# A recurrent layer and an expert attention on one core: maxima halved over partitions, fewer turns, and a first pass beside the projection

## The chip, the core and the metric

The kernel runs on one core of one Trainium2 chip. The metric is the time of one execution on the device, in microseconds; three executions were taken. One further execution was recorded by the hardware profiler. The engines are PE (matrix multiply, with PEld for its weight loads), DVE (vector), ACT (scalar, activations), POOL (GpSimd) and SP (issues transfers). PE writes to PSUM only, which has eight banks; the other data lies in SBUF. Everything is in float32.

## The reference

Two layers, each on normalised input and added to its input. x has the shape 2 x 2048 x 256 (B, T, D).

```python
# layer 1: a plain recurrent layer, h starts at zero
xi = jnp.einsum('btd,hd->bth', x, Wi) + bi
def step(h, xt):
    h_new = jnp.tanh(xt + h @ Wh.T + bh)
    return (h_new, h_new)
...
# layer 2: attention with experts, H = 8 heads of DH = 64, E = 5 experts, 2 chosen
q = (x @ Wq).reshape(b, t, h, dh).transpose(0, 2, 1, 3)
k = (x @ Wk).reshape(b, t, h, dh).transpose(0, 2, 1, 3)
wv = _topk_mask(gl_v, SEL) * jax.nn.sigmoid(gl_v)
xv = jnp.einsum('btd,edk->btek', x, Wv)
v = jnp.einsum('bthe,btek->bhtk', wv, xv)
scores = jnp.einsum('bhid,bhjd->bhij', q * scale, k)
probs = jax.nn.softmax(scores, axis=-1)
attn = jnp.einsum('bhij,bhjd->bihd', probs, v)
out = jnp.einsum('bthe,bthk,ekd->btd', mask_o, attn, Wo)
...
x = x + _L0_attn_ref(_layernorm(x, axis=-1), ...)
x = x + _L0_ffn_ref(_layernorm(x, axis=-1), ...)
```

## The kernel before

**The recurrent layer.** The 2048 steps of a sequence are cut into 128 segments (NS) of 16 steps (S), which run side by side: chunk c holds step c of every segment, for both sequences (B = 2). `measure` takes the norms (DVE), `turn_in` normalises a chunk (POOL) and turns it on PE, `project_in` multiplies it by Wi on PE and writes it with the biases to `xi` (ACT); the input dimension has two halves (KC = 2), so a chunk has two tiles `px`. The loop at L322 puts these in an order written out by hand. Then come two runs over the steps. Run "a" starts every segment from zero at step 3 (SKIP) and keeps only the end states, `ends`; step 3 itself has no matrix product. Run "b" starts every segment from the end state of the one before it, keeps all states in `hs`, and has the residual, the norms and the turning back of the layer beside it (`beside`). In both, `step` (L355) treats the two sequences apart: four products of 128 columns each in two halves, an add of `xi` on DVE, a tanh on ACT. `compare` checks that run b's end states agree with run a's to four units in the last place; if not, a flag makes the kernel run a slow pass over everything.

**The attention.** A unit is one head with 512 queries (QB): 64 units, each in U_T = 4 turns of the loop over T at L1154, each turn with two tiles t of 256 keys (HC = 8 tiles per unit). `scores` writes a tile's scores, 128 x 2 x 512, to two PSUM banks (ps_s, two buffers); `stage` copies them to SBUF (ACT); `largest` takes the running maximum over the tiles (DVE) into `m`. At a unit's seventh tile (c = HC - 2) it folds the two halves of the 256 keys together: `half` in PSUM, then `mm`, 128 x 512 (L663 to L666). What is left is a maximum over 128 partitions: `turn_max` turns `mm` on PE in four pieces, `reduce_max` reduces each (DVE, L684), `spread_max` turns the result back to all partitions on PE (`pt`, L693), and ACT copies it to SBUF (`top`, L699). `subtract` takes it off the staged scores, on DVE from PSUM for a unit's first two tiles, on POOL from SBUF for the other six; `exponential` is ACT; `products` multiplies with the values into the bank `o`; `fold` adds two tiles by a transfer from POOL's queue; `sums` takes the sum over the keys into bank `d`. The subtraction lags the scores by LAG - 1 = 5 turns, the products by 6.

In a turn the engines' order is the order of the calls: exponential of an old tile, scores of two new ones, stage and maximum of each, the subtractions (`fresh` marks the turn with a unit's first two, `sub`), then what the table `before` holds for this turn, the products, the sums, an exponential, and the tables `first_behind` and `behind`; the table `between` is called between the stages and the maxima. `take` brings a finished unit's products to SBUF (ACT copy, DVE add): it is called at the start of the turn after the unit's last products. `close`, `gather` and others finish the unit; `keys` and `queries` of the next head come in `before`, in every unit's third turn.

The values are mixed from five experts per token: `first_experts` projects them for sequence 0 (PE, ACT copy out of a bank: `misc`, which has two buffers, and the bank "d" in turn), `mix` weighs them with the gates and `mix_sum` adds them up (DVE); `experts` projects them for sequence 1 during an earlier head.

Of the kernel before, what the change touches and what calls it, by code (L numbers as in the profile page):

```python
# [14 lines left out]
P = 128  # L15
# [5 lines left out]
def pass_over(  # L21
# [237 lines left out]

    S = NCH  # L260
    NS = P
    NEWTON = 3


# [8 lines left out]

    with tile_pool(name="prep", bufs=3) as pp, tile_pool(
        name="lna", bufs=3
    ) as lnp, tile_pool(name="ps_xi", bufs=3, space=PSUM) as ps_xi, tile_pool(
        name="ps_t", bufs=3, space=PSUM
    ) as ps_t, tc.manual_schedule():
        norm_of, turned = {}, {}

        def measure(c0, n):
            mv = pp.tile([P, n * B, 2], F32, tag=f"mv{n}", name=f"mva{c0}")
            for c in range(c0, c0 + n):
                for b in range(B):
                    stats(lnp, mv[:, (c - c0) * B + b, :], xt[c][:, b, :], f"a{c}_{b}")
            neg, y = scales(lnp, mv, n * B, f"a{c0}")
            for c in range(c0, c0 + n):
                norm_of[c] = neg, y, (c - c0) * B

        def turn_in(c):  # L290
            neg, y, k = norm_of.pop(c)
            xn = pp.tile([P, B, D], F32, tag="xn", bufs=2, name=f"xn{c}")
            tp = ps_t.tile([P, KC, B, P], F32, tag="tp", name=f"tpa{c}")
            for b in range(B):
                normalize(xn[:, b, :], xt[c][:, b, :], neg, y, k + b)
                for kc in range(KC):
                    nc.tensor.transpose(tp[:, kc, b, :], xn[:, b, kc * P : (kc + 1) * P], ident)
            turned[c] = pp.tile([P, KC, B, P], F32, tag="xnT", bufs=2, name=f"xnT{c}")
            nc.scalar.copy(turned[c], tp)

        def project_in(c):
            xnT = turned.pop(c)
            for mc in range(KC):
                px = ps_xi.tile([P, B, P], F32, tag="px", name=f"px{c}_{mc}")
                for kc in range(KC):
                    nc.tensor.matmul(  # L306
                        px.rearrange("p b n -> p (b n)"),
                        lhsT=wi[:, kc, mc * P : (mc + 1) * P],
                        rhs=xnT[:, kc].rearrange("p b n -> p (b n)"),
                        start=kc == 0,  # L310
                        stop=kc == KC - 1,
                    )
                nc.scalar.activation(xi[:, mc, c], px, AF.Identity, bias=bsum[:, mc : mc + 1])

        groups, c0 = [], 0
# [26 lines left out]

    TOL = 4 * 2.0**-23
    GC = NCH // 2
    SKIP = 3
# [6 lines left out]

    def step(nm, s, prev, h, ps_h):  # L355
        for b in range(B):
            if prev is None:
                for mc in range(KC):
                    nc.scalar.activation(h[:, mc, b, :], xi[:, mc, s, b, :], AF.Tanh)
                continue  # L360
            pre = sp.tile([P, KC, NS], F32, tag=f"pre{b}", name=f"pre{nm}_{s}_{b}")
            for mc in range(KC):
                ph = ps_h.tile([P, NS], F32, tag=f"ph{b}_{mc}", name=f"ph{nm}_{s}_{b}_{mc}")
                for kc in range(KC):
                    nc.tensor.matmul(  # L365
                        ph,
                        lhsT=wh[:, kc, mc * P : (mc + 1) * P],
                        rhs=prev(kc, b),
                        start=kc == 0,
                        stop=kc == KC - 1,  # L370
                    )
                nc.vector.tensor_tensor(pre[:, mc, :], ph, xi[:, mc, s, b, :], ALU.add)
                nc.scalar.activation(h[:, mc, b, :], pre[:, mc, :], AF.Tanh)  # L373

    def run(nm, from_zero, keep_states, ps_h, beside=None):
        prev = None if from_zero else (lambda kc, b: ends[:, kc, b, 0:NS])
        for s in range(SKIP if from_zero else 0, S):
            if keep_states:
                h = hs[:, :, s]
            elif s == S - 1:  # L380
                h = ends[:, :, :, 1:]
            else:
                h = sp.tile([P, KC, B, NS], F32, tag="h", name=f"h{nm}_{s}")
# [132 lines left out]
    with tile_pool(name="ps_h", bufs=1, space=PSUM) as ps_h:  # L516
        if slow:
            nc.gpsimd.memset(hs[:, :, S - 1], 0.0)
            with tc.For_i(0, NS, 1):
                nc.vector.tensor_copy(ends[:, :, :, 1:], hs[:, :, S - 1])  # L520
                run("c", False, True, ps_h)
            for c in range(S):
                turn_back(c, "c")
                add_back(c, nc.gpsimd)
# [69 lines left out]
    def first_experts(c):  # L594
# [9 lines left out]
        nc.scalar.copy(xq[:, c % 4], pv.rearrange("p e k -> p k e"))  # L604
        if c % 4 == 3:
# [47 lines left out]
    def largest(t, ss):  # L653
# [8 lines left out]
        half = misc([P, QB], f"mh{u}")  # L662
        nc.vector.tensor_tensor(half, ss[:, 0, :], m[:, 0, :], ALU.max)  # L663
        nc.vector.tensor_tensor(m[:, 1, :], ss[:, 1, :], m[:, 1, :], ALU.max)
        mm_of[u] = ap.tile([P, QB], F32, tag="mm", bufs=1, name=f"mm{u}")
        nc.vector.tensor_tensor(mm_of[u], half, m[:, 1, :], ALU.max)  # L666
        m_of.pop(u)


# [3 lines left out]
        return spare["pool"].tile([P, QB], F32, tag="z", name=nm)  # L673

    def turn_max(u):
        pm = misc([P, QS, P], f"pm{u}")
        mm = mm_of.pop(u)
        for s in range(QS):
            nc.tensor.transpose(pm[:, s, :], mm[:, s * P : (s + 1) * P], ident)
        mx_of[u] = (pm, ap.tile([P, QS], F32, tag="mq", name=f"mq{u}"))  # L680

    def reduce_max(u):
        pm, mq = mx_of[u]
        nc.vector.tensor_reduce(mq, pm, AX.X, ALU.max)  # L684

    def spread_max(u):
        _, mq = mx_of[u]
# [282 lines left out]

    before, between, first_behind, behind = {}, {}, {}, {}

    def at(table, T, f, *a):
        table.setdefault(T, []).append(lambda: f(*a))

# [8 lines left out]
    for i, (b, h) in enumerate(heads):  # L984
# [10 lines left out]
        at(before, T0 + 2, queries, i, 1)  # L995
        for part in range(4):
            if i == 0:
                at(behind, (3, 5, 6, 7)[part], mix, i, part)
                at(behind, (3, 5, 6, 7)[part], mix_sum, i, part)
            else:  # L1000
                T = T0 + U_T * (part - 2) + 2
                at(behind, T - 2, fetch, i, part)
# [1 line left out]
                at(before, T + 1, mix_sum, i, part)  # L1004
        if h == H - 3 and b + 1 < B:
            for c in range(NCH):
                T = T0 + c // 2 * U_T + 1
                at(before if c % 2 else behind, T + c % 2, experts, b + 1, c)
    for b in range(1, B):

# [9 lines left out]
        for c in range(NCH):  # L1020
            T = T0 + c // 2 * U_T + c % 2
            at(behind, T - 2, load_late, b, c)
            at(behind, T, normalize_late, b, c)
            at(behind, T + 2, turn_late, b, c)
            at(behind if c % 2 else before, T + 3, logits_late, b, c)
        T0 += 2 * NCH + U_T
        for part in range(2):
# [15 lines left out]
    for u, (i, n) in enumerate(units):  # L1043
# [10 lines left out]
        if h == H - 1 and (n < NQ - 3 or b < B - 1):  # L1054
            T = T1 + LAG + 4
            for tab, t, f, o, *more in PLACES:
                if T + t < NT:
                    at(tab, T + t, f, b, n * QS + o, *more)

    def drain():  # L1060

# [91 lines left out]
    with tc.manual_schedule():  # L1153
        for T in range(NT):  # L1154
            new = (2 * T, 2 * T + 1)
            sub = [t for t in (2 * (T - LAG + 1), 2 * (T - LAG + 1) + 1) if 0 <= t < 2 * NT]
            old = [t for t in (2 * (T - LAG), 2 * (T - LAG) + 1) if 0 <= t < 2 * NT]
            u_old = (T - LAG) // U_T - 1
            done = (T - LAG) % U_T == 0 and 0 <= u_old < len(units)
            fresh = sub and sub[0] % HC == 0  # L1160
            if done:
                take(u_old)
            if old:
                exponential(old[1])

# [10 lines left out]
            else:  # L1176
# [92 lines left out]
```

## Time and profile before

| | us |
|---|---|
| Three executions | 1551.83, 1552.19, 1552.85 |
| Their median | 1552.19 |
| The profiled execution, its own time | 1552.41 |
| Its span, first to last instruction | 1550.6 |

The mean granted clock of PE was 0.999 of full speed. The page of the profile gives, of the span, how long each engine was busy; a busy PE isn't PE at its peak. These groups of the page belong to the change (line, engine, operation, tiles and shapes, count; busy time and mean ns of one; idle time of the engine just before them and what ended most of it):

```profile
L706 POOL TENSOR_TENSOR p<-p,top 128x1024 f32<-128x1024 f32 x378 | 1009.6, 2780 | 26.2 <-ACT top L699 25.9
L660 DVE TENSOR_TENSOR m<-s,m 128x1024 f32<-128x1024 f32 x320 | 390.9, 1222 | 83.4 <-PE s L638 73.9
L706 DVE TENSOR_TENSOR p<-p,pt 128x1024 f32<-128x1024 f32 x126 | 152.5, 1210 | 0.0
```

By stage, from the time line: the projection runs from 9 to 52 us, run a from 53 to 75, run b to 111, and the first scores come at 121.5. The first unit's maxima are turned at 157.8 and the last one's at 1499.3, which is 21.3 per unit on the mean; the rest is the last units' finish.

### The profile page before, as it was taken

What the parts mean: (1) busy time and instruction counts of PE and PEld (TensorE: products, weight loads), DVE (VectorE), ACT (ScalarE), POOL (GpSimd) and SP (SyncE); (2) the same over time, 40 slices, a digit from 0 to 9 for tenths busy, and PEclk for the clock granted to TensorE, in tenths of its full rate; (3) what the DMA queues carried; (4) which work ended last, traced back from release to release, by engine and by line L of the source; (5) the groups of instructions that cost most, each with busy time, mean ns of one, the idle gap of its engine ahead of it and who ended that gap; (6) DMA issues with size and microseconds to landing.
All of it is one profiled execution on the core that took longest, in us unless ns stands there. A gap on an engine that the chain in (4) does not pass through costs nothing.

```text
span 1550.6 us, 42383 instructions
## 1 busy us (share of the span) xinstructions
PE 1506.5 (97%) x18078; PEld 533.0 (34%) x18078; DVE 1301.1 (84%) x1807; ACT 1242.5 (80%) x1585; POOL 1284.3 (83%) x852
## 2 busy tenths in 40 slices
PE   6999899999999999999999999999999999999997
PEld 5994222222233333333223332222222222222234
DVE  7374899999998888888987778999989999999974
ACT  4674688888888888888887678888888888888872
POOL 3154699999999988999998688899999999999980
PEclk9999999999999999999999999999999999999999
DMA  6021478898888887788797677888888888888965
GB/s 177 1 110 32 116 166 196 188 182 183 181 178 185 185 166 163 169 177 177 165 206 165 166 164 173 173 175 180 176 180 179 175 171 174 174 174 173 208 146 135
DMA packets 87127, 254.52 MB, mean 164 GB/s; under 512 B 11792, under 2 KB 31376, under 8 KB 86928
## 3 DMA queue, kind: packets, MB, share of 16 engines
q0 software_dynamic: 43488, 164.65, 58.0%
q1 hardware_dynamic: 41808, 86.46, 17.0%
q8 instruction: 143, 2.34, 0.6%
q10 hardware_dynamic: 1632, 0.61, 0.2%
q14 instruction: 56, 0.46, 0.1%
HBM read 59.79 MB, written 50.33 MB: 71 GB/s over the span
## 4 chain that ended last, share of the span: by engine, by line
PE 65%; DVE 18%; ACT 7%; issue 5%; DMA 2%; POOL 1%; ACTq 0%; SPq 0%; DVEq 0%; POOLq 0%
PE s L638 22%; PE o L719 18%; DVE m L660 10%; ACT p L650 5%; PE d L740 5%; PE pk L144 3%; PE pq L163 3%; DVE pro L785 3%; PE pz L899 2%; PE phb L365 2%; PE px L306 1%; PE pha L365 1%; DMA p<-p 1%; ACT p L709 1%; PE pv L577 1%
## 5 line engine op out<-in xcount | busy, mean ns | idle before, releaser
L706 POOL TENSOR_TENSOR p<-p,top 128x1024 f32<-128x1024 f32 x378 | 1009.6, 2780 | 26.2 <-ACT top L699 25.9
L650 ACT COPY p<-s 128x1024 f32<-128x1024 f32 x512 | 511.8, 1013 | 143.8 <-issue 59.2
L709 ACT ACTIVATE p<-p 128x1024 f32<-128x1024 f32 x512 | 538.9, 1064 | 49.5 <-DVE p L706 40.5
L638 PE MATMUL s<-q,k 64*32 64x512 f32 x4096 | 501.5, 596 | 4.7 <-ACT p L650 2.4
L638 PE MATMUL s<-qs,k 64*32 64x512 f32 x4096 | 501.5, 596 | 3.4 <-ACT p L650 1.6
L719 PE MATMUL o<-p,v 128*32 128x512 f32 x4096 | 491.6, 597 | 3.2 <-DVE os L756 2.3
L660 DVE TENSOR_TENSOR m<-s,m 128x1024 f32<-128x1024 f32 x320 | 390.9, 1222 | 83.4 <-PE s L638 73.9
L731 POOL DMA_DIRECT2D p<-p x254 | 264.6, 1043 | 94.4 <-issue 40.7
L719 PEld LDWEIGHTS o<-p,v 128*32 128x32 f32 x4096 | 111.8, 109 | 303.8 <-issue 156.6
L638 PEld LDWEIGHTS s<-q,k 64*32 64x32 f32 x4096 | 100.6, 105 | 155.8 <-ACT p L650 59.5
L638 PEld LDWEIGHTS s<-qs,k 64*32 64x32 f32 x4096 | 100.7, 105 | 153.9 <-ACT p L650 58.1
L706 DVE TENSOR_TENSOR p<-p,pt 128x1024 f32<-128x1024 f32 x126 | 152.5, 1210 | 0.0
L740 PE MATMUL d<-p,ones 128*32 128x512 f32 x1032 | 136.8, 592 | 0.7 <-DMA p<-p 0.7
L660 DVE TENSOR_TENSOR m<-s,p 128x1024 f32<-128x1024 f32 x64 | 78.3, 1224 | 47.2 <-ACT p L650 46.2
L785 DVE TENSOR_TENSOR pro<-po,mr 128x1280 f32<-128x1280 f32 (+1 forms) x65 | 95.6, 1471 | 2.6
L622 DVE TENSOR_TENSOR xq<-xq,wp 128x1280 f32<-128x1280 f32 x60 | 89.2, 1487 | 2.1
L628 DVE TENSOR_REDUCE v<-xq 128x256 f32<-128x1280 f32 x60 | 88.5, 1476 | 0.0
L163 PE MATMUL pq<-xn2T,wq 128*32 128x512 f32 x512 | 62.2, 598 | 0.0
L740 PEld LDWEIGHTS d<-p,ones 128*32 128x32 f32 x1032 | 34.1, 110 | 80.2 <-issue 76.9
L144 PE MATMUL pk<-xn2T,wk 128*32 128x512 f32 x512 | 61.5, 598 | 0.0
L835 POOL DMA_DIRECT2D yd<-pro x48 | 60.9, 1268 | 0.0
L400 POOL TENSOR_TENSOR x<-x,hvb 128x512 f32<-128x512 f32 x14 | 17.9, 1275 | 45.8 <-ACT hs L373 34.2
(176 smaller groups left out, 1473.2 us busy)
## 6 DMA issues: line engine op xcount, KB each, us to landing
p<-p POOLq DMA_DIRECT2D x254, 512.0 KB, 5.4
xq<-xvd SPq DMA_DIRECT2D x60, 640.0 KB, 4.6
yd<-pro POOLq DMA_DIRECT2D x48, 640.0 KB, 6.4
qs<-q SPq DMA_DIRECT2D x64, 128.0 KB, 4.4
yd<-pro SPq DMA_DIRECT2D x8, 640.0 KB, 6.3
y<-yd SPq DMA_DIRECT2D x8, 640.0 KB, 6.9
x<-in_x SPq DMA_DIRECT2D x16, 256.0 KB, 6.2
x1d<-x SPq DMA_DIRECT2D x16, 256.0 KB, 2.0
```

What stands on the lines that cost most here:

```text
L144: nc.tensor.matmul(pk[at_col : at_col + 32], lhsT=wk[:, kc, h * DH + g : h * DH + g + 32], rhs=xc[:, kc, c0 // 2 : (c0 + HC) // 2, o, :], ...
L163: nc.tensor.matmul(pq[at_col : at_col + 32, :], lhsT=wq[:, kc, h * DH + g : h * DH + g + 32], rhs=xn2T[:, kc, b, n * QB : (n + 1) * QB], s ...
L622: nc.vector.tensor_tensor(xq, xq, wp.unsqueeze(2).to_broadcast([P, 4, DH, E]), ALU.mult)
L638: nc.tensor.matmul(ss[g : g + 32, o, :], lhsT=k_of[i][half, c, g : g + 32], rhs=q_of[i, n][o][half, :], start=True, stop=True, tile_positi ...
L650: nc.scalar.copy(p, ss)
L660: nc.vector.tensor_tensor(m, ss, ring[t - 1] if c == 1 else m, ALU.max)
L706: eng.tensor_tensor(p, p, top.unsqueeze(1).to_broadcast([P, 2, QB]), ALU.subtract)
L709: nc.scalar.activation(ring[t], ring[t], AF.Exp)
L719: nc.tensor.matmul(o_of[u][at_col : at_col + 32, :], lhsT=v_of[i][:, 2 * c + o, g : g + 32], rhs=ring[t][:, o, :], start=c == 0, stop=c == ...
L731: nc.gpsimd.dma_start(out=ring[t], in_=ring.pop(t + 1), accum_op=ALU.add)
L740: nc.tensor.matmul(den_of[u][32 * g : 32 * (g + 1), :], lhsT=ones32, rhs=ring[(t, t1)[g // 2]][:, g % 2, :], start=first, stop=last, tile_ ...
L785: nc.vector.tensor_tensor(dst, po[:, s : s + n, 0:DH].unsqueeze(1).to_broadcast([P, E, n, DH]), mr[:, s : s + n].rearrange("p s e -> p e s ...
```

## The change

It has five parts.

1. The maximum over the keys is written back to `m`, and then halved over the partitions: two maxima of 64 partitions x 256 columns put the upper 64 partitions against the lower, one for each half of the queries, into a tile `mm` of 128 x 256. `turn_max` then turns two pieces instead of four, and the reduction reads half as much.
2. In the turn with a unit's first subtractions, the second running maximum comes before the first subtraction, but for the turns in a set `crowded`, which keep the old order: the first 16, those with a turn of late input or of the output, and one near the end.
3. `take` is called in the turn of the unit's last products, ahead of the exponential at its end, and no longer at the start of the next turn.
4. `first_experts` goes round three banks ("o" is the third); the first head's mixes and sums come earlier or in other tables; the experts of the second sequence come two units later.
5. Run a is no longer run by itself. `first_run(c)` does its step c behind the projection of chunk c + 1: it adds Wh times the last state to the projection's tile `px`, which still lies in PSUM, for both sequences at once (256 columns), and takes the tanh with the biases from there. `px` has six buffers of a bank each; `turn_in` uses `misc`.

```diff
-            tp = ps_t.tile([P, KC, B, P], F32, tag="tp", name=f"tpa{c}")
+            tp = misc([P, KC, B, P], f"tpa{c}")
...
+        def first_run(c):
+            pxs, prev = px_of.pop(c), h_of.pop(c - 1, None)
+            if slow or c < SKIP:
+                return
+            h = ends[:, :, :, 1:]
+            if c < S - 1:
+                h = pp.tile([P, KC, B, NS], F32, tag="h", bufs=2, name=f"ha_{c}")
+            for mc, px in enumerate(pxs):
+                for kc in range(KC if prev is not None else 0):
+                    nc.tensor.matmul(
+                        px,
+                        lhsT=wh[:, kc, mc * P : (mc + 1) * P],
+                        rhs=prev[:, kc],
+                        start=False,
+                        stop=kc == KC - 1,
+                        skip_group_check=True,
+                    )
+                nc.scalar.activation(h[:, mc], px, AF.Tanh, bias=bsum[:, mc : mc + 1])
+            h_of[c] = h
...
             if c >= 2:
                 project_in(c)
+            if c:
+                first_run(c - 1)
+        first_run(NCH - 1)
...
-                run("a", True, False, ps_h)
-                run("b", False, True, ps_h, beside)
+                run("b", ps_h, beside)
...
-        pv = ps_o.tile([P, E, DH], F32, tag="d", name=f"pvf{c}") if c % 2 else misc([P, E, DH], f"pvf{c}")
+        tag = (None, "o", "d")[c % 3]
+        pv = ps_o.tile([P, E, DH], F32, tag=tag, name=f"pvf{c}") if tag else misc([P, E, DH], f"pvf{c}")
...
-        mm_of[u] = ap.tile([P, QB], F32, tag="mm", bufs=1, name=f"mm{u}")
-        nc.vector.tensor_tensor(mm_of[u], half, m[:, 1, :], ALU.max)
+        nc.vector.tensor_tensor(m[:, 1, :], half, m[:, 1, :], ALU.max)
+        mm_of[u] = ap.tile([P, QB // 2], F32, tag="mm", bufs=1, name=f"mm{u}")
+        for o in range(2):
+            cols = slice(o * QB // 2, (o + 1) * QB // 2)
+            nc.vector.tensor_tensor(
+                mm_of[u][o * DH : (o + 1) * DH], m[0:DH, 1, cols], m[DH:P, 1, cols], ALU.max
+            )
...
-        pm = misc([P, QS, P], f"pm{u}")
+        pm = misc([P, QS // 2, P], f"pm{u}")
...
-        for s in range(QS):
+        for s in range(QS // 2):
             nc.tensor.transpose(pm[:, s, :], mm[:, s * P : (s + 1) * P], ident)
...
-        nc.vector.tensor_reduce(mq, pm, AX.X, ALU.max)
+        nc.vector.tensor_reduce(
+            mq.rearrange("p (o s) -> p s o", o=2), pm.rearrange("p s (o k) -> p s o k", o=2), AX.X, ALU.max
+        )
...
-                at(behind, (3, 5, 6, 7)[part], mix, i, part)
-                at(behind, (3, 5, 6, 7)[part], mix_sum, i, part)
+                at(between if part == 1 else behind, (2, 4, 5, 6)[part], mix, i, part)
+                at(between if part % 2 else behind, (2, 4, 6, 8)[part], mix_sum, i, part)
...
-                T = T0 + c // 2 * U_T + 1
+                T = T0 + c // 2 * U_T + 2 * U_T + 1
...
-            if done:
-                take(u_old)
...
-            if fresh:
+            if fresh and T in crowded:
                 subtract(sub[0])
             if T % U_T:
                 largest(new[0], ss[0])
+            if fresh and T not in crowded:
+                subtract(sub[0])
             if fresh:
                 subtract(sub[1])
...
+            if k >= 0 and k % U_T == U_T - 1:
+                take(k // U_T)
             if sub:
                 exponential(sub[0])
```

More of the change, by code (lines that the diff above doesn't have):

```diff
@@ L261, in pass_over @@
     NS = P
+    SKIP = 3
     NEWTON = 3
@@ L275, in pass_over @@
         name="lna", bufs=3
[L276 to L279, printed above, removed]
+    ) as lnp, tile_pool(name="ps_xi", bufs=6, space=PSUM) as ps_xi, tc.manual_schedule():
+        norm_of, turned, px_of, h_of = {}, {}, {}, {}
         def measure(c0, n):
@@ L302, in project_in @@
             xnT = turned.pop(c)
+            px_of[c] = []
             for mc in range(KC):
-                px = ps_xi.tile([P, B, P], F32, tag="px", name=f"px{c}_{mc}")
+                px = ps_xi.tile([P, 512], F32, tag="px", name=f"px{c}_{mc}")[:, : B * P]
                 for kc in range(KC):
                     nc.tensor.matmul(
-                        px.rearrange("p b n -> p (b n)"),
+                        px,
                         lhsT=wi[:, kc, mc * P : (mc + 1) * P],
@@ L312, in project_in @@
                     )
+                px = px.rearrange("p (b n) -> p b n", b=B)
                 nc.scalar.activation(xi[:, mc, c], px, AF.Identity, bias=bsum[:, mc : mc + 1])
+                px_of[c].append(px)
+        def first_run(c):
[8 more added lines that the diff above has]
+                    nc.tensor.matmul(
+                        px,
+                        lhsT=wh[:, kc, mc * P : (mc + 1) * P],
[6 more added lines that the diff above has]
+            h_of[c] = h
         groups, c0 = [], 0
@@ L332, in pass_over @@
                 project_in(c)
+            if c:
+                first_run(c - 1)
+        first_run(NCH - 1)
     TOL = 4 * 2.0**-23
     GC = NCH // 2
-    SKIP = 3
     sp = rw.enter_context(tile_pool(name="step", bufs=3))
@@ L356, in step @@
         for b in range(B):
[L357 to L360, printed above, removed]
             pre = sp.tile([P, KC, NS], F32, tag=f"pre{b}", name=f"pre{nm}_{s}_{b}")
@@ L373, in step, with run @@
                 nc.scalar.activation(h[:, mc, b, :], pre[:, mc, :], AF.Tanh)
[L375 to L383, printed above, removed]
+    def run(nm, ps_h, beside=None):
+        prev = lambda kc, b: ends[:, kc, b, 0:NS]
+        for s in range(S):
+            h = hs[:, :, s]
             step(nm, s, prev, h, ps_h)
@@ L520, in pass_over @@
                 nc.vector.tensor_copy(ends[:, :, :, 1:], hs[:, :, S - 1])
-                run("c", False, True, ps_h)
+                run("c", ps_h)
             for c in range(S):
@@ L971, in pass_over @@
     before, between, first_behind, behind = {}, {}, {}, {}
+    crowded = set(range(4 * U_T))
     def at(table, T, f, *a):
@@ L1024, in pass_over @@
             at(behind, T + 2, turn_late, b, c)
+            crowded.add(T + 2)
             at(behind if c % 2 else before, T + 3, logits_late, b, c)
@@ L1056, in pass_over @@
             for tab, t, f, o, *more in PLACES:
+                crowded.add(T + t)
                 if T + t < NT:
                     at(tab, T + t, f, b, n * QS + o, *more)
+    crowded.add(NT - 3)
     def drain():
@@ L1157, in pass_over @@
             old = [t for t in (2 * (T - LAG), 2 * (T - LAG) + 1) if 0 <= t < 2 * NT]
-            u_old = (T - LAG) // U_T - 1
-            done = (T - LAG) % U_T == 0 and 0 <= u_old < len(units)
             fresh = sub and sub[0] % HC == 0
-            if done:
-                take(u_old)
             if old:
```

## The prediction

> **What bounds the kernel now.** I read the page first, then the busy time by stretch, then the time line of one unit (one head, 512 queries), engine by engine, and last the waits.
>
> ```profile
> PE 1506.5 (97%) x18078; PEld 533.0 (34%) x18078; DVE 1301.1 (84%) x1807; ACT 1242.5 (80%) x1585; POOL 1284.3 (83%) x852
> 30.00:40.00 10.00, 9.96 (x57) 8.54 (x56) 6.80 (x33) 6.78 (x14) 6.49 (x12) 1.00 0.01 2
> 40.00:50.00 10.00, 10.00 (x57) 8.85 (x55) 0.00 (x0) 7.14 (x15) 3.29 (x6) 1.00 0.00 1
> 266.10:286.40 20.30, 20.22 (x244) 5.82 (x236) 19.49 (x26) 17.63 (x21) 17.82 (x11) 1.00 0.72 162
> 717.80:740.30 22.50, 22.17 (x276) 6.97 (x268) 19.47 (x26) 19.18 (x24) 22.34 (x20) 1.00 0.81 169
> 1054.00:1074.30 20.30, 20.22 (x244) 5.82 (x236) 18.37 (x22) 17.64 (x21) 18.75 (x12) 1.00 0.87 179
> ```
>
> The columns after the stretch are its length, then PE, PEld, DVE, ACT, POOL busy, clock, DMA. PE is full both in the projection (30 to 50) and in the units, at full clock. But behind it stand, by unit, a DVE that is nearly full (19.49 of 20.30 at 266) or a POOL that is (22.34 of 22.50 at 718). A regular unit, on PE:
>
> ```profile
> 1054.03 0.66 PE L679 MATMUL pm<-ident,mm 128*128 128x128 f32 x4
> 1054.62 1.92 PE L719 MATMUL o<-p,v 128*32 128x512 f32 x16
> 1056.47 0.65 PE L693 MATMUL pt<-ident,mq 128*128 128x128 f32 x4
> 1056.96 0.60 PE L772 MATMUL po<-ident,os 128*128 128x128 f32 x4
> ...
> 1062.55 0.61 PE L638 MATMUL s<-q,k 64*32 64x512 f32 x4
> ...
> 1063.27 0.63 PE L638 MATMUL s<-q,k 64*32 64x512 f32 x4
> ...
> 1074.33 0.65 PE L679 MATMUL pm<-ident,mm 128*128 128x128 f32 x4
> ```
>
> From pm to pm is 20.30. Groups of scores follow each other at 0.43 to 0.45, but 1062.55 to 1063.27 is 0.72: PE stands 0.27 there, because the bank is still read by a maximum that DVE does after a subtraction. The rows of the trace have such a step in 41 units (9.7 us). The same unit on DVE:
>
> ```profile
> 1052.88 1.48 DVE L628 TENSOR_REDUCE v<-xq 128x256 f32<-128x1280 f32 x1
> 1054.39 0.69 DVE L763 TENSOR_TENSOR os<-d,os 64x512 f32<-64x512 f32 x1
> 1055.10 0.69 DVE L684 TENSOR_REDUCE mq<-pm 128x4 f32<-128x512 f32 x1
> ...
> 1071.85 0.68 DVE L664 TENSOR_TENSOR m<-s,m 128x512 f32<-128x512 f32 x1
> 1072.57 0.69 DVE L666 TENSOR_TENSOR mm<-mh,m 128x512 f32<-128x512 f32 x1
> 1073.18 1.48 DVE L628 TENSOR_REDUCE v<-xq 128x256 f32<-128x1280 f32 x1
> ```
>
> mm ends at 1073.26 and PE turns it at 1074.33: 1.07 to spare. The reduction ends at 1055.79 and PE spreads it at 1056.47: 0.68 to spare, of which 0.62 are usable, since where PE does wait here it starts 0.06 after the reduction.
>
> **The turns.** Four turns of 0.273 take 0.60 (the po row), so one more costs (0.60 - 0.273) / 3 = 0.109. Two fewer: -0.22 a unit, on the engine that is full.
>
> **The halving.** The last 128x512 maximum stays (it goes into m). New are two maxima of 64x256. A row of 256 columns on DVE is 0.42 (L909), and 64 partitions instead of 128 change nothing (L763 0.69 against L666 0.69). Where the output changes its half, rows don't overlap: L628 ends at 1054.36 and L763 starts at 1054.39; elsewhere the next starts 0.08 before the end (1073.18). So: from the last 128x512 maximum to what follows it was 0.61, and becomes 0.72 + 0.45 + 0.45 = 1.62, +1.01. If all rows overlap it is +0.81. The reduction reads 256 instead of 512 columns, 0.42 for 0.69: -0.27. DVE pays +0.74 a unit (+0.54 at best); I take 0.74, by the row that changes its half as these do. What is late next: mm comes 0.90 later with 1.07 to spare, so the turns don't wait. What DVE holds behind it (L628, L763, the reduction) comes 0.74 later, PE is there 0.22 earlier: 0.62 - 0.22 = 0.40 to spare, so PE waits 0.34 for the spread (0.14 at best). Cover gone, the halving costs PE its whole 0.74.
>
> **Maxima ahead.** In a unit's first turn of subtractions the second maximum goes before the first subtraction instead of behind it, outside the crowded turns. Its bank is free some 1.2 earlier, so the 0.27 goes. The subtraction, and the exponential behind it on ACT, come 1.2 later; ACT stood 0.73 at just that place (waiting for DVE), the moved copy of `take` (0.57) now fills it, and PE needs that exponential only after the next scores and a projection of keys or queries (1.7): nothing.
>
> **Sum by unit.** A regular unit: -0.22 - 0.27 + 0.34 = -0.15. Of the 41 units with the stall, 7 (from 225 to 367) have a full DVE: 19.49 + 0.74 = 20.23 of 20.30, so PE gains and DVE takes it: 0. The other 34: -5.1. In 5 units (at 183 and four between 628 and 782) PE already waits for the reduction; the 0.74 goes straight through: +3.7. Of the other 18, 14 have 0.95 or more to spare before the spread: -0.20 each, -2.8; four have 0.68 and no stall at the scores: -0.22 + 0.34, +0.5 in all. Together -3.7.
>
> **Start.** Three banks instead of two for the first values:
>
> ```profile
> 146.66 3.44 PE L577 MATMUL pvf<-wv,xn2T 128*32 128x320 f32 x48 [1.08 <-ACT q L173]
> 154.73 1.28 PE L577 MATMUL pvf<-wv,xn2T 128*32 128x320 f32 x16 [0.47 <-ACT xf L604]
> 169.14 1.28 PE L577 MATMUL pvf<-wv,xn2T 128*32 128x320 f32 x16 [1.62 <-ACT xf L604]
> ```
>
> Each is PE waiting for a copy out of a bank: -3.2 (between 0 and -3.2; PE is full around them, so I take all). The first mixes go one turn earlier, where DVE stands (it waits 3 to 8 us at a time between 122 and 165); before the unit at 183 PE waits 0.5 and 1.2 for that queue: between 0 and -1.7, I take -1.0. The later experts move by two units, PE work of the same size: 0, unless they land on POOL's full units.
>
> **The run beside the projection.** It looks like the large term: the run takes from 52.2 to 74.65. But PE is full in both. Run a is 12 steps of 16 matmuls of 128 columns in 21.5 us, 1.79 each; a step becomes 8 of 256 columns, which the projection does in 1.73 (33.57 to 35.30). 12 x 0.06 = 0.7, and 0.9 between the stages go; at the end PE waits for two last tanh, 0.3 and 0.5. Steps with matmuls start only behind chunk 5, at about 30.7, when PE has stopped waiting for normalised input. So 0.8 - 0.9 - 0.7, -0.8. Its 48 adds (14 us of DVE) go, but they lay beside PE. ACT has per chunk a copy, two identities and now two tanh, 0.59 + 4 x 0.47 = 2.5, in 3.9 of PE: hidden.
>
> **The port.** The two halves are maxima with both inputs in SBUF; today's DVE rows in the units have one in PSUM. POOL subtracts beside them (2.69 each, two in a row at this place). The nearest rows:
>
> ```profile
> 119.03 1.11 POOL L217 TENSOR_SCALAR xn2d<-x,rootd 128x256 f32<-128x256 f32 x1
> 119.11 0.67 DVE L506 TENSOR_TENSOR off<-hs,ends 128x512 f32<-128x512 f32 x1
> ```
>
> Such a DVE row beside POOL kept its 0.67, and POOL's went from 0.56 (L217 of xn2b) to 1.11. So I let DVE pay nothing and POOL 2 x 0.42 = 0.85 a unit: a regular unit has 20.30 - 18.75 = 1.55 of it. From the other side: the four DVE scalings just before it, also beside POOL, took 0.41 to 0.65, so DVE can wait; at most one whole subtraction, 2.69.
>
> The Trainium skill (SBUF — State Buffer, Who interferes with whom) speaks against the change: a DVE instruction with two SBUF inputs and a GpSimd one that reads SBUF exclude each other, and whichever issues second blocks until the first is done. By it the halves, which come up in the middle of a subtraction, would wait; then the sum is that of the third case below. By the row it is POOL that waits.
>
> **Sum.** -3.7 - 3.2 - 1.0 - 0.8 = -8.7 against the profiled run of 1552.41 (span 1550.6; the median of the runs shown is 1552.19): 1543.7.
>
> **Cases.** (1) As summed, 1543.7, its own range 1535 to 1550: 0.55. (2) The halves overlap and fit: every unit gets -0.22, the 41 stalls go, nothing waits for the spread: 64 x 0.22 + 9.7 and the start's 5.0, -28.8, 1523.6. For it: where DVE idles (0.77 and 0.66 in the regular unit) delays are swallowed. Against: the queue between mm and the reduction has no idle time. 0.16. (3) Slower: the halves wait for POOL's running subtraction, on the mean half of 2.69 = 1.35. mm comes 0.90 + 1.35 = 2.25 later with 1.07 to spare: PE stands 1.18, less 0.22 + 0.27, +0.69 x 64 = +44: 1596. It decides from a wait of 0.17 + 0.49 = 0.66 a unit. For it the slowed scalings, against it L506. 0.16. (4) POOL pays the 0.85 also in some ten units where it is full (718 above): +8.5 on case 1, 1552: 0.11. (5) The changed rounding of the run makes the comparison at its end ask for the slow pass: several times the time; against it, the rounding moves by a last place and the tolerance is four. 0.02.
>
> About 0.2% (3.1 us) can be told from no change. Faster: case 2 and nearly all of case 1, 0.69; same: case 4 and the rest of case 1, 0.13; slower: cases 3 and 5, 0.18. The range goes from case 2 to just beyond case 4, 1523 to 1556, and leaves out case 3, 5 and the ends.
>
> **What would show it.** Turns: two rows of pm instead of four a unit. Stall: no 0.72 step between scores. Halving: two rows of 0.42; their length, and POOL's subtraction beside them, settle the port; the spread starting 0.06 after the reduction settles the 0.34. The run: PE full from 30 on, its end at about 73.8. I am wrong if the halves last over 0.7, or if a regular unit is over 20.3 or under 19.85.

## The result, and the profile after

The kernel after takes 1870.68 us (median of 6 runs, 1854.94 to 1872.97); the kernel before took 1552.52 beside it. The ratio is 1.202 [1.198, 1.206]: slower by 318 us, far outside the range. The profiled run took 1870.68, its span is 1868.9, and the mean granted clock of PE fell from 0.999 to 0.916.

The page first: the busy times, and the groups of the halves and of the products.

```profile
PE 1613.5 (86%) x17854; PEld 558.3 (30%) x17854; DVE 1569.6 (84%) x1887; ACT 1245.6 (67%) x1559; POOL 1285.8 (69%) x852
L687 DVE TENSOR_TENSOR mm<-m 64x256 f32<-64x256 f32 x128 | 286.7, 2240 | 4.4
L745 PE MATMUL o<-p,v 128*32 128x512 f32 x4096 | 576.2, 686 | 4.5 <-DVE os L782 4.4
```

Two things are wrong at once. A half takes 2.24 on the mean where 0.42 was expected. And PE has 224 matmuls fewer and yet is busy 107 us longer: the products alone take 576.2 instead of 491.6 us, though nothing about them was changed. The waits say where PE and ACT stand:

```profile
PE pm L702 <- DVE mm L687: 204.4, 59, 6.1
ACT top L725 <- PE pt L719: 318.9, 63, 11.3
```

(total, times, longest): PE waits 59 times for the halves, 3.5 each. The time line of one unit, PE first, then DVE, then POOL:

```profile
1227.94 1.92 PE L745 MATMUL o<-p,v 128*32 128x512 f32 x16
...
1231.99 0.61 PE L655 MATMUL s<-q,k 64*32 64x512 f32 x4
1235.95 0.44 PE L702 MATMUL pm<-ident,mm 128*128 128x128 f32 x2 [3.35 <-DVE mm L687]
1236.32 3.59 PE L745 MATMUL o<-p,v 128*32 128x512 f32 x16
1239.85 0.65 PE L719 MATMUL pt<-ident,mq 128*128 128x128 f32 x4
```

```profile
1230.76 0.69 DVE L683 TENSOR_TENSOR m<-mh,m 128x512 f32<-128x512 f32 x1
1231.49 4.41 DVE L687 TENSOR_TENSOR mm<-m 64x256 f32<-64x256 f32 x2
1235.93 1.49 DVE L645 TENSOR_REDUCE v<-xq 128x256 f32<-128x1280 f32 x1
```

```profile
1229.57 0.88 POOL L757 DMA_DIRECT2D p<-p  x1 [0.20 <-issue]
1230.18 4.97 POOL L732 TENSOR_TENSOR p<-p,top 128x1024 f32<-128x1024 f32 x2
1238.75 0.88 POOL L757 DMA_DIRECT2D p<-p  x1 [3.60 <-issue]
```

POOL does two subtractions that follow each other at once, from 1230.18 to 1235.15. The halves come up 1.3 after the first one's start; the first half takes 3.95 and ends at 1235.44, 0.3 after the **second** subtraction; the second half then takes 0.42. Over all 64 units, counted in the rows: the first half ends 0.3 to 0.5 after the last of two subtractions in 58, of more than two POOL operations in five, and one unit is free of it. The 1.92 of the products after it becomes 3.59, and the windows around that stand (length, then PE, PEld, DVE, ACT, POOL busy, clock, DMA) say why:

```profile
1225.00:1235.90 10.90, 7.60 (x100) 1.79 (x92) 10.38 (x9) 10.71 (x12) 9.95 (x6) 1.00 0.85 173
1235.90:1240.00 4.10, 4.05 (x19) 0.94 (x20) 3.82 (x4) 0.07 (x1) 0.88 (x1) 0.58 0.39 116
1240.00:1250.00 10.00, 10.00 (x124) 3.25 (x127) 8.66 (x11) 7.17 (x9) 8.01 (x5) 1.00 0.73 136
```

After the stand the granted clock is 0.58 on the mean over 4.1 us, then 1.00 again. The clock records show 62 stretches at half clock, 317 us together (before: one, 4.6 us, at the very end). So the 318 us are, on PE: 239.9 of gaps between matmuls instead of 27.7 (+212), and 1613.5 busy instead of 1506.5 (+107).

### The profile page after: what moved, and what is told of

It is laid out like the page before. It is cut to its first block, busy times and chain, and to the rows that moved or that the text cites. A ratio compares the mean times of both kernels' runs of the same rounds, so it can differ in the third digit from the quotient of the medians.

```text
span 1868.9 us, 41973 instructions
## 1 busy us (share of the span) xinstructions
PE 1613.5 (86%) x17854; PEld 558.3 (30%) x17854; DVE 1569.6 (84%) x1887; ACT 1245.6 (67%) x1559; POOL 1285.8 (69%) x852
## 4 chain that ended last, share of the span: by engine, by line
PE 60%; DVE 35%; issue 3%; ACT 1%; DVEq 0%; ACTq 0%
PE o L745 20%; PE s L655 16%; DVE mm L687 15%; DVE m L677 7%; PE pq L163 3%; PE pt L719 3%; PE pk L144 2%; PE d L766 2%; DVE m L683 2%; DVE mh L680 2%; DVE m L681 2%; PE po L798 2%; PE pz L925 2%; PE pm L702 2%; PE phb L387 1%
## 5 line engine op out<-in xcount | busy, mean ns | idle before, releaser
L732 POOL TENSOR_TENSOR p<-p,top 128x1024 f32<-128x1024 f32 x378 | 997.0, 2713 | 84.5 <-ACT top L725 72.4
L745 PE MATMUL o<-p,v 128*32 128x512 f32 x4096 | 576.2, 686 | 4.5 <-DVE os L782 4.4
L655 PE MATMUL s<-q,k 64*32 64x512 f32 x4096 | 496.0, 598 | 3.6 <-ACT p L667 2.8
L757 POOL DMA_DIRECT2D p<-p x254 | 238.9, 942 | 333.8 <-issue 212.7
L687 DVE TENSOR_TENSOR mm<-m 64x256 f32<-64x256 f32 x128 | 286.7, 2240 | 4.4
L725 ACT COPY top<-pt 128x512 f32<-128x512 f32 x63 | 36.9, 585 | 318.9 <-PE pt L719 318.9
L745 PEld LDWEIGHTS o<-p,v 128*32 128x32 f32 x4096 | 122.5, 119 | 348.4 <-issue 218.2
L702 PE MATMUL pm<-ident,mm 128*128 128x128 f32 x128 | 37.9, 391 | 217.7 <-DVE mm L687 204.4
L702 PEld LDWEIGHTS pm<-ident,mm 128*128 128x128 f32 x128 | 16.2, 177 | 274.8 <-DVE mm L687 213.2
L800 DVE TENSOR_REDUCE den<-po 128x4 f32<-128x8 f32 x64 | 10.7, 166 | 92.6 <-PE po L798 92.5
```

The source lines that it names most:

```text
L655: nc.tensor.matmul(ss[g : g + 32, o, :], lhsT=k_of[i][half, c, g : g + 32], rhs=q_of[i, n][o][half, :], start=True, stop=True, tile_positi ...
L687: nc.vector.tensor_tensor(mm_of[u][o * DH : (o + 1) * DH], m[0:DH, 1, cols], m[DH:P, 1, cols], ALU.max)
L732: eng.tensor_tensor(p, p, top.unsqueeze(1).to_broadcast([P, 2, QB]), ALU.subtract)
L745: nc.tensor.matmul(o_of[u][at_col : at_col + 32, :], lhsT=v_of[i][:, 2 * c + o, g : g + 32], rhs=ring[t][:, o, :], start=c == 0, stop=c == ...
L757: nc.gpsimd.dma_start(out=ring[t], in_=ring.pop(t + 1), accum_op=ALU.add)
```

## The experiments

The theory: the halves have both inputs in SBUF and are shut out while POOL subtracts, for as long as POOL goes from one subtraction to the next; and the stand that this makes costs PE half its clock behind it. Rivals: the change of partition half costs the time (the output lies in other partitions than an input), some other part of the change is to blame, and the slow products have a cause of their own.

**One input in PSUM.** The kernel after, but the last maximum is made in two pieces, the upper 64 partitions in PSUM, so that each half has one input in PSUM.

```diff
-        nc.vector.tensor_tensor(m[:, 1, :], half, m[:, 1, :], ALU.max)
+        nc.vector.tensor_tensor(half[DH:P], half[DH:P], m[DH:P, 1, :], ALU.max)
+        nc.vector.tensor_tensor(m[0:DH, 1, :], half[0:DH], m[0:DH, 1, :], ALU.max)
...
-                mm_of[u][o * DH : (o + 1) * DH], m[0:DH, 1, cols], m[DH:P, 1, cols], ALU.max
+                mm_of[u][o * DH : (o + 1) * DH], half[DH:P, cols], m[0:DH, 1, cols], ALU.max
```

> The changed kernel, but each halved maximum has one input in PSUM: the upper 64 partitions are first brought together in PSUM, the lower 64 in SBUF (one 128x512 maximum becomes two of 64x512, about 0.7 us more DVE a unit). Theory (a DVE instruction with two SBUF inputs waits for POOL's subtractions): the halves take 0.42 us each and don't wait, PE stands at most 0.6 us a unit before the turns, the clock stays over 0.98, 1540 to 1575 us. Rival (reading one half of the partitions and writing the other is slow in itself): halves still over 1 us on the mean, time over 1750.

Measured 1596.1, ratio 1.029 [1.027, 1.030], above what was expected. Each half takes 0.43 beside the same POOL subtractions, no gap on PE is over 2 us, the clock is 0.997. What is left is a DVE queue that is longer by the halves and one more maximum of 0.7: DVE is busy 1378.6, and PE waits for it at both places, a little each time:

```profile
PE pm L703 <- DVE mm L688: 30.4, 51, 1.0
PE pt L720 <- DVE mq L709: 26.3, 56, 1.5
```

**The old maxima.** All of the change but the halving. Against the kernel after:

```diff
-        nc.vector.tensor_tensor(m[:, 1, :], half, m[:, 1, :], ALU.max)
...
+        mm_of[u] = ap.tile([P, QB], F32, tag="mm", bufs=1, name=f"mm{u}")
+        nc.vector.tensor_tensor(mm_of[u], half, m[:, 1, :], ALU.max)
...
+        for s in range(QS):
...
+        nc.vector.tensor_reduce(mq, pm, AX.X, ALU.max)
```

> The changed kernel with the old end of the maxima: one 128x512 maximum with an input in PSUM, four turns, the full reduction. All else of the change stays. Theory: the loss goes whole, what is left is the order of the maxima (about 41 stalls of 0.24 us, 9.7 us) and the start (0 to 5 us): 1535 to 1545. Rival (the later subtraction, the moved copy or the run beside the projection bear part of the loss): over 1570.

Measured 1538.76, ratio 0.992 [0.990, 0.993]. It is faster than both kernels, and its page shows PE full again:

```profile
PE 1498.7 (98%) x17982; PEld 540.0 (35%) x17982; DVE 1290.7 (84%) x1759; ACT 1233.9 (80%) x1559; POOL 1282.5 (83%) x852
```

Against it the kernel after loses 331.9 us, which PE's rows give again: gaps 239.9 instead of 22.0, busy 1613.5 instead of 1498.7, together +332.7.

**The halving alone**, put into the kernel before: those lines the other way round, the change's first part.

```diff
-        nc.vector.tensor_tensor(mm_of[u], half, m[:, 1, :], ALU.max)
+        nc.vector.tensor_tensor(m[:, 1, :], half, m[:, 1, :], ALU.max)
...
+                mm_of[u][o * DH : (o + 1) * DH], m[0:DH, 1, cols], m[DH:P, 1, cols], ALU.max
```

> The kernel before with the halving alone (two maxima of 64x256 with both inputs in SBUF, two turns, the halved reduction). Theory: the whole loss is in it, 1850 to 1900, the first half about 4 us a unit, clock about 0.92. Rival (it needs the new order around it): under 1700.

Measured 1879.75, ratio 1.211 [1.209, 1.213], with 60 stretches at half clock (289.9 us). The whole loss lies in this part.

**Both inputs in SBUF, same partitions.** The kernel before with one line changed: `half` goes into `m` instead of PSUM, so that the old last maximum of 128 x 512 has both inputs in SBUF. No halving, no change of partitions.

```diff
-        half = misc([P, QB], f"mh{u}")
+        half = m[:, 0, :]
```

> The kernel before, where only the first of the last three maxima is written to SBUF and no longer to PSUM, so that the last, 128x512, has both inputs in SBUF, in the same partitions; no halving, four turns. Theory (the port): this one row waits for POOL's two subtractions, 3 to 4.5 us on the mean in place of 0.69, and the time is 1750 to 1900. Rival (crossing partitions is what is slow): the row stays at 0.69 and the time at 1552.

Measured 1858.85, ratio 1.198 [1.194, 1.201]. That maximum by source line (least, median and greatest ns of one), and one unit's DVE and POOL rows:

```profile
L666 DVE TENSOR_TENSOR mm<-m x64: 693/4952/6898, 154.3 to 1793.3; 128x512 f32<-128x512 f32 x64
```

```profile
1052.47 6.39 DVE L666 TENSOR_TENSOR mm<-m 128x512 f32<-128x512 f32 x1
```

```profile
1052.80 5.51 POOL L706 TENSOR_TENSOR p<-p,top 128x1024 f32<-128x1024 f32 x2
```

0.69 in the kernel before, a median of 4.95 here (a mean of 5.03, more than expected), and two subtractions waited for in 55 of 64 units (in this one the rest of an earlier one as well): the input's place alone does it. Crossing partitions isn't the cause.

**The turns behind the products.** The kernel after; PE should have 1.9 of products to do while it waits.

```diff
-                if T > 0:
-                    turn_max(T // U_T - 1)
-                    reduce_max(T // U_T - 1)
...
+            if T > 0 and T % U_T == 0:
+                turn_max(T // U_T - 1)
+                reduce_max(T // U_T - 1)
             if 3 <= k and k % 2:
```

> The kernel after, with the turns of the halved maxima and their reduction called behind the turn's products instead of ahead of them: PE has 1.9 us of ready products to do while it waits for the halves. Theory (the wait costs twice, once as the stand and once because a stand of over 3 us is followed by about 5 us at half clock): the first half still waits about 3.95 us, but PE stands only some 1.4 us, there are next to no stretches of low clock, the products of 16 take 1.92 again everywhere, PE's busy time goes back to about 1495, and the time to 1600 to 1690. Rival (the low clock comes from something else in the change, the products' group of 16 or the load on the units' queues): slow stretches stay near 60, PE's busy time stays near 1600 and the time above 1750.

Measured 1990.81, ratio 1.283 [1.280, 1.285]: as a cover it failed. The stand before the turns fell to 1.55, but the reduction now stands behind another maximum on DVE, and PE waits for it at the spread:

```profile
1231.53 0.44 PE L702 MATMUL pm<-ident,mm 128*128 128x128 f32 x2 [1.55 <-DVE mm L687]
1235.35 1.11 PE L719 MATMUL pt<-ident,mq 128*128 128x128 f32 x4 [3.38 <-DVE mq L708]
...
1240.46 1.93 PE L745 MATMUL o<-p,v 128*32 128x512 f32 x16
```

The stretches at half clock (64) and PE's busy time (1636.2) stayed where the rival had them, but so did a long stand, so they don't tell the two apart. The run still settles one thing. The products come ahead of the long stand here, and their time is normal; the scores, which come behind it, have become slow (598 ns in the kernel after):

```profile
L655 PE MATMUL s<-q,k 64*32 64x512 f32 x4096 | 573.7, 680 | 3.5 <-ACT p L667 2.8
...
L745 PE MATMUL o<-p,v 128*32 128x512 f32 x4096 | 495.4, 601 | 4.9 <-DVE os L782 4.3
```

What is slow is what follows the stand, whatever it is.

**POOL stops for the halves**, between the two subtractions of the turn, by a small copy that reads the halves.

```diff
+    def yield_port(u):
+        junk = ap.tile([P, 1], F32, tag="junk", bufs=1, name=f"junk{u}")
+        nc.gpsimd.tensor_copy(junk, mm_of[u][:, 0:1])
...
             if sub and not fresh:
+                if T % U_T == U_T - 1 and T < NT - 1:
+                    yield_port(T // U_T)
                 subtract(sub[1])
```

> The kernel after, with one small copy on POOL (one column of the halved maxima) between the two subtractions of the turn in which a unit's maxima are halved, so that the second subtraction comes behind the halves. Theory (a DVE operation with two SBUF inputs that finds POOL at work is not served between two POOL operations that follow each other at once, so it waits for both): the first half now waits for one subtraction only, 0.4 to 2.7 us in place of 3.95, PE's stand falls to 0.5 to 1.5, the low clock is gone for the most part, and the time is 1570 to 1660; POOL's second subtraction comes about 1 later. Rival (the wait is as long as POOL's queue, whatever is in it, or the later subtraction makes POOL and then ACT the late ones): the halves stay at 3 us or more, or PE waits for ACT's exponentials instead; 1750 or more.

Measured 1753.2, ratio 1.130 [1.128, 1.132]: the rival's time, by its second reading (POOL and then ACT late, PE waiting for the exponentials). The halves took 0.45 on the mean: all but one of the 64 units' found POOL at rest, since POOL was early and stood for them, 5.19 in the unit shown. So the copy moved the wait to POOL, ACT's exponential came late, and PE stood there:

```profile
1145.45 0.18 POOL L736 COPY junk<-mm 128x1 f32<-128x1 f32 x1 [5.19 <-DVE mm L687]
```

```profile
1149.08 1.91 PE L749 MATMUL o<-p,v 128*32 128x512 f32 x8 [2.24 <-ACT p L739]
```

```profile
1146.80:1149.08 2.28, 0.04 (x4) 0.00 (x0) 1.14 (x3) 1.08 (x2) 2.28 (x3) 1.00 0.58 166
1149.08:1152.70 3.62, 3.62 (x16) 1.75 (x16) 1.23 (x1) 3.42 (x4) 3.62 (x2) 0.53 0.92 221
1152.70:1156.00 3.30, 3.30 (x49) 0.98 (x52) 3.06 (x5) 1.97 (x3) 3.30 (x3) 1.00 0.41 78
```

Another cause, a shorter stand, and the clock falls all the same. This run has nothing to say on two subtractions or one, but it shows the clock apart from the port.

**The same copy one subtraction later**, behind `subtract(sub[1])`.

> The kernel after, with the small copy on POOL (one column of the halved maxima) one subtraction later than in e6_pool_yields: behind the subtraction that the halves meet, ahead of the next one, which followed at once. Theory (a waiting DVE operation is served only when POOL stops issuing; so what costs 3.95 is one rest of a subtraction and one whole subtraction): the first half ends 0.3 after that one subtraction, so it takes 0.4 to 2.7, 1.4 to 1.7 in a regular unit; PE's stand is under 2.0 and the low clock is gone; 1570 to 1660. Rival (a DVE operation waits for a fixed time or for the second subtraction whatever stands between): the half stays at 3 us or more, and the time above 1750.

Measured 1614.31, ratio 1.040 [1.038, 1.041]. In 58 units POOL again was done before the halves came. Five met a subtraction behind which the copy now stood, and there the first half ended about 0.3 after that one subtraction (it took 0.54 to 1.90). In one unit, at 1554.9, no copy stood between, two subtractions followed each other, and the half took 4.03. One of the five, POOL then DVE:

```profile
198.16 2.88 POOL L732 TENSOR_TENSOR p<-p,top 128x1024 f32<-128x1024 f32 x1
201.85 0.19 POOL L736 COPY junk<-mm 128x1 f32<-128x1 f32 x1 [0.81 <-DVE mm L687]
```

```profile
199.44 2.36 DVE L687 TENSOR_TENSOR mm<-m 64x256 f32<-64x256 f32 x2
```

The subtraction ends at 201.04; the first half, begun at 199.44, ends at 201.34. The price of 1.4 to 1.7 "in a regular unit" was wrong, since a regular unit's halves met no POOL work; the wait for one, where POOL stops, was right, though on five units only. This kernel is 75.5 us behind the one with the old maxima, and PE stands 73 us longer. The larger share that the profile names is on POOL's side: its subtractions come late, and so do ACT's exponentials, for which PE waits. The next is DVE's longer queue: PE waits 21.9 for the reduction, 2.1 with the old maxima (waits in total, times, longest):

```profile
POOL junk L736 <- DVE mm L687: 134.8, 62, 3.9
ACT p L739 <- POOL p L732: 129.4, 118, 2.1
PE o L749 <- ACT p L739: 41.4, 53, 1.3
PE pt L719 <- DVE mq L708: 21.9, 48, 1.4
```

**The other parts, each alone in the kernel before.** Their lines are in the diff of the change; here the one that names each. The run:

```diff
-                run("a", True, False, ps_h)
+                first_run(c - 1)
```

> The kernel before, with the first run beside the projection alone. By the prediction's sum -0.8 (PE is full in both), so 1551.2 against 1552.0. Rival (the run's 21.5 us come off the end): under 1535. A third reading, from the second run's start in the kernel with the old maxima (73.1 instead of 74.65): -1.5.

Measured 1551.44, ratio 0.9998 [0.9989, 1.0007]: no gain that can be told from none, and no large one.

The maxima ahead:

```diff
-            if fresh:
+            if fresh and T in crowded:
                 subtract(sub[0])
             if T % U_T:
                 largest(new[0], ss[0])
+            if fresh and T not in crowded:
+                subtract(sub[0])
```

> The kernel before, with the second maximum ahead of the first subtraction in the turns that aren't crowded, alone. By the prediction the stall of 0.27 at the scores goes in 41 units, 9.7 us in all: 1542 to 1544, since 7 of these units have a full DVE. Rival (the subtraction 1.2 later makes ACT's exponential late and PE waits there instead): 1550 or more.

Measured 1563.87, ratio 1.007 [1.006, 1.009]: slower. The step of 0.72 between scores is gone (2 units instead of 41), but the exponential on ACT, which waits 1.40 for the subtraction, and `take`'s copy behind it hold the staging, and PE stands at the next scores:

```profile
1069.32 1.06 ACT L709 ACTIVATE p<-p 128x1024 f32<-128x1024 f32 x1 [1.40 <-DVE p L706]
1070.28 0.56 ACT L755 COPY os<-o 64x512 f32<-64x512 f32 x1
```

```profile
1073.97 0.63 PE L638 MATMUL s<-q,k 64*32 64x512 f32 x4 [0.42 <-ACT p L650]
```

`take` earlier:

```diff
-            if done:
-                take(u_old)
...
+            if k >= 0 and k % U_T == U_T - 1:
+                take(k // U_T)
```

> The kernel before, with take called in the turn of a unit's last products instead of at the start of the next one, alone. The prediction let it stand at nothing: 1552. If the parts alone make up what the kernel with the old maxima gained (13.3), and the others come as predicted (0.8, 8 to 9.7 and 4.2), it is within 1 of 1552; a rival is that ACT's copy, now ahead of the exponential, holds PE's next products: 1555 or more.

Measured 1552.92, ratio 1.0005 [0.9996, 1.0013]: nothing.

These last two together:

> The kernel before, with two parts: take called earlier and the second maximum ahead of the first subtraction. Alone the first gave +1.3 and the second +12.3, and yet the kernel with the old maxima, which has both and the start (-7.8) and the run (-0.2), gained 13.3. Theory (the later subtraction makes ACT's exponential late, and the exponential with the copy of take behind it holds the staging and so the next scores by 0.42 in a unit; with the copy ahead of the exponential it lies in time that ACT stands anyway): the pair gives 13.3 - 7.8 - 0.2 = 5.3 less than before, 1546 to 1547.5. Rival (the parts act by themselves and the kernel with the old maxima has its gain from the start with the run): 1562 to 1566.

Measured 1551.13, ratio 0.9991 [0.9982, 1.0000]: the loss of 12 is gone, as the theory had it, but the gain is 1.6 and not 5.3. A regular unit at 1070 is 20.10 long instead of 20.30. By the times from one unit's turns to the next, the profiled run gains 4.6 between 900 and 1400, and loses 1.7 between 200 and 500, where DVE is full in part, and 2.9 elsewhere: as a whole it is as long as the profiled run before.

And the start:

```diff
+        tag = (None, "o", "d")[c % 3]
...
+                T = T0 + c // 2 * U_T + 2 * U_T + 1
```

> The kernel before, with the start alone: three banks for the first experts' values, the first head's mixes and sums earlier, the later experts two units later. By the prediction -3.2 for the banks and -1.0 for the mixes: 1547.8. Rival (PE only waits later, at the first unit): 1552.

Measured 1543.85, ratio 0.995 [0.993, 0.996]: more than expected. PE's three stands for a bank (1.26, 0.63, 1.78; what the step between two starts has beyond the usual one) are gone, two of the stands around the unit at 183 (0.60, 1.23) too, and three by the later experts at 566 to 591 (0.54, 0.20, 0.54). These three aren't all that the later experts give: the two profiled runs are 10.1 apart, of which 5.0 come before the turns of the unit at 225 and 5.1 in the units from 558 to 900.

The parts' ratios multiply to 0.9935, the kernel with the old maxima has 0.9918 [0.9904, 0.9931]. The 2.6 us between them can't be told from the sum of these intervals.

## Why the prediction was wrong

**The port: the step that failed.** I wrote "I let DVE pay nothing and POOL 2 x 0.42", by one row (L506, 0.67 beside a POOL row of 1.11). That row differs from the halves in two things: the two operations had started within 0.08 of each other, and POOL's was a scaling with one tensor input. Here POOL is in the middle of a subtraction, which has two, when the halves come. DVE paid 3.53 (3.95 - 0.42) in nearly every unit, and POOL's subtractions nothing (their median is 2.68 after, 2.69 before). Which of the two differences decides isn't shown. The Trainium skill (SBUF — State Buffer, Who interferes with whom), which I set against my row, was right for the subtractions: with two SBUF inputs beside GpSimd's reads, the one that issues second blocks. (The row itself doesn't fit it: POOL starts first there, and POOL's is the longer one.) The skill says that the second blocks until the first finishes; the runs here show more, that the blocked operation also sits through a second subtraction that follows at once.

**Case 3 had the mechanism and the wrong size.** It took half of one subtraction, 1.35, and gave my bound from above as one whole, 2.69. With the measured 3.53 its own formula gives 0.90 + 3.53 - 1.07 = 3.36 of stand; 3.35 was measured. By it the time would have been 1552 + 64 x (3.36 - 0.49) = 1736 (it takes the stall's 0.27 in all 64 units, though 41 have it; that is 6 us).

**The rest was in no case.** The remaining 135 us are for the most part what the half clock costs: PE is busy 114.8 us longer than with the old maxima, with 128 matmuls fewer (317 us at half clock lose up to 158). Every sum in the prediction priced PE's work at its durations of before.

**Right:** two turns take 0.44 instead of 0.66; a half takes 0.42 when it is free, the reduction 0.42; from the last 128 x 512 maximum to what follows the halves is 1.71 where POOL is at rest (1.62 predicted). The stall at the scores goes, and `take` fills ACT's stand, without which that part loses 12. The run beside the projection is no large term (-0.8 predicted, between -1.7 and +1.1 measured), and the slow pass wasn't asked for. **Mis-sized:** maxima ahead, with `take`, give -1.6 where I had put the whole stall's gain in 34 units: the units between 900 and 1400 give 4.6, and others, those with a full DVE among them, give most of it back. The start gives -7.8 for -4.2: the banks' stands are -3.7 for -3.2, the mixes' -1.6 for -1.0 (two of 0.60 and 1.23 go, one grows by 0.19), and the later experts, which I had at nothing, give -5.1 in the profiled run, of which the three stands are 1.3; where the rest comes from isn't shown. And if rows overlapped by the 0.08 that I read, the halving's best case was +0.68 on DVE, not +0.81; nothing above hangs on it.

**Open:** why a waiting DVE operation isn't served between two POOL subtractions isn't shown, only that it isn't. What the halving would give without the port was not measured by itself, since each kernel that freed it (an input in PSUM, a stop on POOL) added work or a wait. In the one that stops POOL later, the wait for the spread is 0.46 in 48 units; 0.34 was predicted for a regular one.

## What to carry to other kernels

Before a DVE operation with two tensor inputs is added beside a busy POOL, look where its inputs lie: with one in PSUM it cost 0.43 beside subtractions, with both in SBUF 3.95. Price a stand of PE not by its length alone: if it can pass some 2 us, add 3.41 us or more at half clock (how often, the last section says). And read a single favourable row for the order in which the two engines came, and for the kind of operation on either side, before taking it as the price.

## What the runs showed of the hardware

A waiting DVE operation with two SBUF inputs is passed over between two POOL subtractions that follow each other at once: two waited for in 58 of 64 units here, 55 of 64 in the kernel with the 128 x 512 maximum; one only where POOL stopped behind it (five units). That holds for subtractions, which have two tensor inputs, not for every POOL operation: in 13 of the 58 units an operation with one tensor input (L217, L251 or L254) follows the second subtraction as closely, and the half is served ahead of it. POOL, then DVE, in one of them:

```profile
641.08 4.99 POOL L732 TENSOR_TENSOR p<-p,top 128x1024 f32<-128x1024 f32 x2
645.79 0.97 POOL L217 TENSOR_SCALAR xl<-xl,rootl 128x256 f32<-128x256 f32 x1
```

```profile
642.38 4.67 DVE L687 TENSOR_TENSOR mm<-m 64x256 f32<-64x256 f32 x2
```

The second subtraction ends at 646.07, and the first half 0.29 later, at 646.36. Here it is POOL that pays: the scaling takes 0.97, and 0.56 where nothing holds it.

The granted clock halves in or behind a stand of PE, for 3.41 us or a multiple of it. The changes lie on a grid: in each of the seven runs that have such stretches from the first units on, they are whole multiples of 3.4133 us apart, to 0.001 us (but for the end of the run). What decides, in all these traces, is how much of one such step PE stands, by the gaps between its rows, whose ends are modelled. From 150 us to 20 us before the end, at full clock, all 259 steps with over 2.01 us of gaps are followed by half clock, and none of 2630 with under 1.89; between these it is 18 of 26. At half clock, all 123 steps with over 0.60 keep it, and all 268 with under 0.47 end it. So a stand's length alone doesn't decide: where POOL stops between its two subtractions, 45 of the 58 stands from 1.94 to 2.29 brought half clock; with the 128 x 512 maximum 13 of 48 stands of 2.5 to 3.2 didn't, each cut by the grid into two parts of at most 2.01. The Trainium skill (TensorE: Matmul & The Clock Gate, Part 1: The HAM clock gate) puts the fall after an idle window of about 3.4 us; some 1.9 to 2.0 us of standing in a step of that length were enough here.
